# Feed-forward of one decoder layer: four more block pairs of up by two levels of block sums, and one-level pairs summed in PSUM

## The chip, the core and the metric

The kernel runs on one core of a Trainium2 chip. The time is that of the device for one execution, in microseconds (us). Before: a median of 1256.03 us over three runs (1255.54 to 1256.44). One further execution was profiled; every row of a profile or trace below is from it.

## The reference

One decoder layer on x of 1024 rows by 512 features, all in fp32: attention with 32 query heads and 8 key and value heads of 128 features, and then a gated feed-forward network with 1792 inner features. A normalisation follows each.

```python
x = layernorm(x + attention(x, wq, wk, wv, wo))
nx = x * rsqrt(mean(x * x) + 1e-5) * ln_w
g, u = nx @ gate_w.T, nx @ up_w.T          # 1024 x 1792 each
x = layernorm(x + (silu(g) * u) @ down_w.T)
```

## The kernel before

Attention comes first and takes the span up to about 1004 us. The change touches none of its instructions. What follows is the feed-forward part.

**Data.** `nT` holds the normalised rows turned, so that the 512 features lie on partitions (four chunks of 128) and the 1024 rows along the free axis. `hT[k]` holds inner features k x 128 to k x 128 + 127 for all rows: 14 blocks, first gate's output, then SiLU of it, then its product with up. `res` holds the rows before normalisation, in parts of the tiles `sums0` to `sums3`; the rest of these tiles serves as room for sums.

**One level.** The product of weights and `nT` is cut in two along each of three axes and computed with seven block products in place of eight (Strassen-Winograd). `blocks(m, ...)` loads the weights of inner block m and of block m + 7 (`far`), and GpSimd forms four sums of weight blocks. `lower` computes products 4 and 5 into the two banks of one tile of PSUM (`pair`, here `pb`), and `strassen` the other five. In the kernel before, each of these five has a bank of its own (`mbank`, four buffers): ScalarE copies product 1 to SBUF, and VectorE makes the four outputs of a pair of blocks with seven additions. A product is two matmuls of 128 x 128 x 512, each two instructions. The operands on the side of the rows are `s1` to `s4`, made on VectorE.

**Two levels.** `unit_blocks(m, ...)` loads the weights of four inner blocks (m, m + 1, m + 7, m + 8). GpSimd forms the sums of both levels. Each of the seven outer products, in the order k = 1, 2, 6, 7, 5, 3, 4, is a generator `stages` with seven matmuls of 128 x 128 x 256 in four steps. Step one fills a bank `c`, which ScalarE copies into `a` (both halves) and into `v`. Step two adds two products onto `a`, and ScalarE copies a half of `a` to `b`. Step three adds a third, and ScalarE copies that to the other half of `b`. Step four adds the last two, and VectorE sums `a`, `b` and `v` into `hT` or into four kept sums (`sa`, `sb`, `ua`, `ub`). Two of each three stages keep `a` and `b` in a `pair` tile, the third in two `mbank` tiles. The loop interleaves stages: step one of stage n, step two of n - 1, step four of n - 2, step three of n - 1. The operands on the side of the rows are in `x2`, which `inner_sums` fills on VectorE.

**Order.** Block 0 (with block 7) comes first, by one level, for gate and for up (`first_lower`, then `strassen` twice), while the last rows are still being normalised (`turn_norm`). Then gate's blocks follow in three units by two levels (m = 1, 3, 5). Then up's blocks follow in six pairs by one level (m = 1 to 6). In each pair ScalarE applies SiLU to gate's outputs after its copy of product 1, and GpSimd and VectorE multiply them by up. In pair 1 VectorE also scales `res` (eight operations, line 1518). From pair 2 on the weights of down are loaded, and GpSimd forms their sums (`weigh_rows`). Down comes last, by one level.

TensorE's instructions run in the order of the program (`keep_in_program_order`). A scheduler orders the other engines' queues as the kernel is built. Each engine works through its queue in order.

The rows of the profile name lines of the kernel before. Line 137 is the helper `matmul`. Lines 1111 (turned rows to `nT`), 1318 to 1328 (`strassen`), 1348 to 1350 (s2, s3, s4), 1369 to 1372 (`inner_sums`), 1414 to 1442 (`stages`), 1201 to 1245 (sums of weights), 1501 (SiLU) and 1503 (product with up) are those the text uses.

Of the kernel before, what the change touches and what calls it, by code (L numbers as in the profile page):

```python
# [28 lines left out]
F32 = mybir.dt.float32  # L29
# [67 lines left out]
def kernel(  # L97
# [47 lines left out]
    def mbank(name):  # L145
        return ps_m.tile([P, W], F32, tag="mbank", name=name)
# [4 lines left out]
    def rows(name):  # L151
        return wp.tile([P, W], F32, tag="w", bufs=3, name=name)

    def two_rows(name):
        return wp.tile([P, T], F32, tag="ww", bufs=4, name=name)
# [21 lines left out]
    mvs = const.tile([P, NT, 2], F32, tag="mvs", name="mvs")  # L177
    rs = const.tile([P, 2, NT], F32, tag="rs", name="rs")
# [7 lines left out]
    with ExitStack() as att:  # L186
# [494 lines left out]
        def pin(ins):  # L681

            if draining:
                tc.keep_in_program_order(ins)
# [419 lines left out]

        def turn_norm(k, n):
            i = ORDER[k]
            pt = mbank(f"nt_ps{i}").rearrange("p (c t) -> p c t", c=NC)
            for c in range(NC):
                turn(pt[:, c, :], n[:, c * P : (c + 1) * P])
            pin(  # L1110
                nc.vector.tensor_tensor(
                    nT[:, :, i * P : (i + 1) * P],
                    pt,
                    lnw.unsqueeze(2).to_broadcast([P, NC, P]),
                    ALU.mult,
                )
            )

# [52 lines left out]
    with ExitStack() as ffn:  # L1171
# [77 lines left out]
        def product(out, w, x):  # L1249
            for c in range(half):  # L1250
                matmul(
                    out,
                    lhsT=w[:, c, :],
                    rhs=x[:, c, :],
                    start=(c == 0),
                    stop=(c == half - 1),
                )
            return out
# [42 lines left out]
        kept_in = copied = None  # L1301

        def strassen(m, k, w, p5, p4, c11, c12, c21, c22):
            nonlocal copied
            b11, b21, b22, u1, u2, u3, u4 = w
            u = f"{k}_{m}"

            def bank(name):
                return mbank(f"{name}{u}")

            def kept(tag):
                if kept_in is None:
                    return rows(f"{tag}{u}")
                return kept_in.tile([P, W], F32, tag=tag, name=f"{tag}{u}")

            p1, p2 = product(bank("p1"), b11, a11), product(bank("p2"), b21, a12)
            v, v4 = kept("v"), kept("v4")
            copied = nc.scalar.copy(v, p1)
            nc.vector.tensor_tensor(c11, p2, v, ALU.add)
            p6 = product(bank("p6"), u2, s2)  # L1320
            nc.vector.tensor_tensor(v, p6, v, ALU.add)
            nc.vector.tensor_tensor(v4, p5, v, ALU.add)
            p7 = product(bank("p7"), u3, s3)
            nc.vector.tensor_tensor(v, p7, v, ALU.add)
            nc.vector.tensor_tensor(c22, p5, v, ALU.add)
            nc.vector.tensor_tensor(c21, v, p4, ALU.subtract)
            p3 = product(bank("p3"), b22, s4)
            nc.vector.tensor_tensor(c12, p3, v4, ALU.add)
# [25 lines left out]
        strassen(0, "g", wg, *pg, *hs)  # L1354
        for h in hs:
            nc.scalar.activation(h, h, AF.Silu)
        us = [fp.tile([P, T], F32, tag=f"h{k}", name=f"u{k}_0") for k in (6, 12)]
        us = [u[:, ts] for u in us for ts in (t0, t1)]
        strassen(0, "u", wu, *pu, *us)


# [3 lines left out]
        def inner_sums(r, to):  # L1365
            r11, r12 = r[:, :, 0, left], r[:, :, 0, right]
            r21, r22 = r[:, :, 1, left], r[:, :, 1, right]
            k1, k2, k3, k4 = (x2[:, to, k, :] for k in range(4))
            nc.vector.tensor_tensor(k1, r12, r11, ALU.subtract)
            nc.vector.tensor_tensor(k2, r22, k1, ALU.subtract)  # L1370
            nc.vector.tensor_tensor(k3, r22, r12, ALU.subtract)
            nc.vector.tensor_tensor(k4, r21, k2, ALU.subtract)

        by_half = nT.rearrange("p (n c) t -> p n c t", c=half)
        inner_sums(by_half[:, :, :, t0], slice(0, 2))
        inner_sums(ns[:, :4].rearrange("p n (c t) -> p n c t", c=half), slice(3, 7))
        inner_sums(by_half[:, 1:, :, t1], slice(2, 3))
# [8 lines left out]
        for h, u in zip(hs, us):  # L1386
            nc.gpsimd.tensor_tensor(h, h, u, ALU.mult)


        def stages(n, m, k, w, kept):  # L1390
# [28 lines left out]
            nc.scalar.copy(b[:, left], a[:, right])  # L1419
# [12 lines left out]
            def into(to_a, to_b, of_a, of_b):  # L1432
                add(to_a, a, of_a)
                add(halves(to_b), halves(of_b), twice(v))
                add(to_b, b, to_b)
# [4 lines left out]

            if k == 1:
                nc.scalar.copy(sa, a)
                add(halves(sb), halves(b), twice(v))
            elif k == 2:
                into(*h(0, t0), sa, sb)
            elif k == 6:
                into(sa, sb, sa, sb)
            elif k == 7:
                into(ua, ub, sa, sb)
            elif k == 5:  # L1450
                into(sa, sb, sa, sb)
                into(*h(1, t1), ua, ub)
            elif k == 3:
                into(*h(1, t0), sa, sb)
            else:
                into(*h(0, t1), ua, ub)
# [3 lines left out]
        inner = []  # L1460
        for m in (1, 3, 5):
            if m < 5:
                units.append(unit_blocks(m + 2, gate_t))
            for k in (m, m + 1, m + far, m + far + 1):
                hidden(k)
            for k in (1, 2, 6, 7, 5, 3, 4):
                inner.append(stages(len(inner), m, k, units[m // 2][k], kept))
                for back in (0, 1, 2, 1):
                    if back < len(inner):
                        next(inner[-1 - back])  # L1470
# [7 lines left out]
        kept_in = gp  # L1478
        wd, us = [], []
# [3 lines left out]
        def weigh_rows(c):  # L1483

            (b11, b12), (b21, b22) = ((w[:, :OH], w[:, OH:]) for w in (wd[c], wd[c + NI // 2]))
            u1, u2, u4 = (room.pop() for _ in range(3))
            nc.gpsimd.tensor_tensor(u1, b12, b11, ALU.subtract)
            nc.gpsimd.tensor_tensor(b12, b22, b12, ALU.subtract)
            nc.gpsimd.tensor_tensor(u2, b22, u1, ALU.subtract)
            nc.gpsimd.tensor_tensor(u4, b21, u2, ALU.subtract)  # L1490
            us.append((b11, b21, b22, u1, u2, b12, u4))

        for m in range(1, far):
            wu = blocks(m, "u", up_t)
            pu = lower(m, "u", wu)
            hs = [hT[k][:, ts] for k, ts in at(m)]
            ups = [gp.tile([P, W], F32, tag=f"g{n}", bufs=1, name=f"u{n}_{m}") for n in range(4)]
            strassen(m, "u", wu, *pu, *ups)
            with tc.issue_after(copied.ins):
                for h in hs:  # L1500
                    nc.scalar.activation(h, h, AF.Silu)
            for n, (h, u) in enumerate(zip(hs, ups)):
                (nc.gpsimd, nc.vector)[n % 2].tensor_tensor(h, h, u, ALU.mult)
            if m == 2:
                for t in [two_rows(f"wd{k}") for k in range(4)] + [piece(f"wd{k}") for k in (4, 5, 6)]:
                    wd += [t[:, :W], t[:, W:]]
                with tc.issue_after(loaded.ins):
                    for k in range(NI):
                        c = k // 2 + k % 2 * NI // 2
                        nc.sync.dma_start(wd[c], down_t[c * P : (c + 1) * P, :])  # L1510
            with tc.issue_after(summed.ins):
                for c in range((m - 2) * 2, (m - 1) * 2):
                    if 0 <= c < NI // 2:
                        weigh_rows(c)
            if m == 1:
                for k, i in enumerate(ORDER):
                    tc.keep_in_program_order(
                        nc.vector.tensor_scalar(
                            res[i],
                            res[i],  # L1520
                            mvs[:, k, 0:1],
                            rs[:, 0, k : k + 1],
                            ALU.subtract,
                            ALU.mult,
                        )
                    )
# [4 lines left out]
        for i in range(NT // 2):  # L1531
# [16 lines left out]
            def kept(tag):  # L1548
                bufs = 1 if tag == "v2" else None
                return gp.tile([P, W], F32, tag=tag, bufs=bufs, name=f"{tag}d{i}")[:, :OH]  # L1550
# [3 lines left out]
            p1s, v2, v4 = kept("v"), kept("v2"), kept("v4")  # L1554
# [118 lines left out]
```

## Time and profile before

| | |
|---|---|
| Median of three runs | 1256.03 us (1255.54 to 1256.44) |
| Profiled execution: time, span of its instructions | 1255.41 us, 1253.2 us |
| TensorE, VectorE, ScalarE, GpSimd busy in that span | 1235.6, 926.1, 491.8, 503.2 us |
| Mean granted clock of TensorE | 0.999 of full speed |
| Block 0, first matmul of `strassen` to the last | 1004.95 to 1022.38 us |
| Gate in units of two levels | 1022.38 to 1089.34 us |
| Up in pairs of one level | 1089.34 to 1161.44 us |
| Down, to the end of the span | 1161.44 to 1253.2 us |

In the rows PE is TensorE, DVE VectorE, ACT ScalarE, POOL GpSimd and PEld TensorE's weight load. A row of the timeline has the start, the duration, the engine, the line, the operation, output<-input and the count of instructions; in brackets stands the idle time of the engine before it and who ended it. A row of a matmul group covers its instructions from the first start to the last end, and the next group may start before that end, since matmuls are pipelined. A row of the waits has the engine that waited, what for, the time in total, how often, and the longest. A row of a window has the stretch, its length, the busy time and count of each engine, TensorE's granted clock, and the share and rate of the DMA engines.

### The profile page before, as it was taken

Reading aid. Unit: us, or ns where it says so; the run is one execution under the profiler, and the core shown is the slowest. Engines: PE = TensorE matmul, PEld = TensorE weight load, DVE = VectorE, ACT = ScalarE, POOL = GpSimd, SP = SyncE. Lnnn points to the kernel's source line nnn. Section 1 sums busy time; section 2 is a strip of 40 time slices with the busy share of each in tenths; the row PEclk is TensorE's granted clock in tenths of the full one; section 3 lists DMA queues with packets and bytes.
Section 4 is the critical chain, followed back from the end, with each engine's and each line's share of the span. In section 5 each row is a group of like instructions: output and inputs, shape, how many; then the busy total and the mean of one; then the engine's idle time right before and its main releaser. Section 6 shows DMA issues by size and latency. Waiting matters only on the chain. (4 is left out here: it accounts for less than half of the span.)

```text
span 1253.2 us, 14678 instructions
## 1 busy us (share of the span) xinstructions
PE 1235.6 (99%) x4252; PEld 754.9 (60%) x4252; DVE 926.1 (74%) x1876; ACT 491.8 (39%) x1000; POOL 503.2 (40%) x734
## 2 busy tenths in 40 slices
PE   9999999999999999999999999999999999999998
PEld 5645575565456755655567556554656758744887
DVE  5866887787788767877797678777765787577743
ACT  0443344444443444444444444454555135412000
POOL 4641434342424233425341424244320886386321
PEclk9999999999999999999999999999999999999999
DMA  8243325433444344334433433444444301510000
GB/s 277 51 118 80 84 65 145 103 88 79 130 97 100 79 119 100 93 82 123 99 86 85 131 83 84 120 117 110 112 103 113 92 17 36 167 51 1 17 18 34
DMA packets 86159, 115.56 MB, mean 92 GB/s; under 512 B 18368, under 2 KB 57024, under 8 KB 86080
## 3 DMA queue, kind: packets, MB, share of 16 engines
q1 hardware_dynamic: 85072, 112.66, 35.8%
q10 hardware_dynamic: 1008, 1.97, 0.4%
q8 instruction: 34, 0.56, 0.2%
q14 instruction: 45, 0.37, 0.1%
HBM read 37.23 MB, written 2.10 MB: 31 GB/s over the span
## 5 line engine op out<-in xcount | busy, mean ns | idle before, releaser
L609 ACT ACTIVATE p<-s,low 128x928 f32<-128x928 f32 (+31 forms) x256 | 179.1, 700 | 375.4 <-DVE low L589 363.2
L617 DVE STREAM_TRANSPOSE turned<-p 128x1024 f32<-128x1024 f32 (+7 forms) x244 | 187.3, 776 | 103.7 <-ACT p L614 70.8
L137 PE MATMUL o<-moved,v 128*128 128x512 f32 x550 | 254.6, 594 | 0.0
L614 ACT ACTIVATE p<-p,share 128x928 f32<-128x928 f32 (+31 forms) x256 | 188.0, 735 | 119.1 <-DVE share L613 119.0
L589 DVE CUSTOM_DVE_ANT_0 s<-s,mask 128x928 f32<-128x928 f32 (+31 forms) x256 | 179.1, 700 | 36.8 <-PE s L137 35.3
L137 PE MATMUL s<-k,queries 128*128 128x512 f32 (+15 forms) x576 | 204.0, 463 | 2.1 <-ACT p L609 2.1
L137 PEld LDWEIGHTS s<-k,queries 128*128 128x128 f32 x576 | 108.4, 190 | 110.5 <-issue 97.8
L137 PEld LDWEIGHTS o<-moved,v 128*128 128x128 f32 x550 | 102.4, 190 | 102.2 <-issue 95.1
L137 PE MATMUL q_p<-blocks,wq 128*128 128x512 f32 x260 | 124.5, 594 | 0.0
L604 POOL MEMSET p<- 128x96 f32 (+2 forms) x192 | 26.8, 150 | 229.4 <-DVE turned L617 208.6
L417 POOL TENSOR_TENSOR queries<-queries,q_b 128x512 f32<-128x512 f32 x52 | 71.4, 1372 | 114.9 <-DVE queries L416 106.0
L137 PE MATMUL y<-wo,oT 128*128 128x256 f32 x428 | 105.0, 382 | 0.7 <-ACT oT L847 0.7
L137 PEld LDWEIGHTS y<-wo,oT 128*128 128x128 f32 x428 | 79.4, 190 | 22.8 <-issue 7.9
L613 DVE RECIPROCAL share<-total 128x1 f32<-128x1 f32 x256 | 40.0, 156 | 61.3 <-ACT p L609 59.0
L411 DVE TENSOR_TENSOR q_b<-queries,sin 64x512 f32<-64x512 f32 x104 | 83.0, 798 | 3.1
L137 PEld LDWEIGHTS q_p<-blocks,wq 128*128 128x128 f32 x260 | 48.4, 190 | 45.9 <-issue 40.2
L137 PE MATMUL s<-kT,queries 128*128 128x512 f32 (+8 forms) x192 | 68.7, 466 | 1.9 <-ACT p L609 1.8
L772 DVE TENSOR_TENSOR sums<-y,sums 128x512 f32<-128x512 f32 x112 | 66.9, 606 | 3.5 <-PE y L137 2.3
L137 PEld LDWEIGHTS s<-kT,queries 128*128 128x128 f32 x192 | 35.7, 190 | 37.7 <-issue 28.9
L137 PE MATMUL y<-u,os 128*128 128x256 f32 x224 | 55.5, 384 | 0.7 <-POOL os L751 0.6
L137 PE MATMUL q_p<-blocks,uq 128*128 128x512 f32 x104 | 49.7, 592 | 0.0
L609 ACT ACTIVATION_READ_ACCUMULATOR p<-s,low 128x1 f32 x256 | 49.5, 193 | 0.0
(340 smaller groups left out, 1911.0 us busy)
## 6 DMA issues: line engine op xcount, KB each, us to landing
moved<-turned SPq DMA_DIRECT2D x112, 128.0 KB, 2.4
moved<-turned SPq DMA_DIRECT2D x128, 112.0 KB, 2.2
moved<-turned SPq DMA_DIRECT2D x112, 96.0 KB, 2.2
moved<-turned SPq DMA_DIRECT2D x112, 80.0 KB, 2.1
wo<-wo SPq DMA_DIRECT2D x16, 512.0 KB, 4.4
moved<-turned SPq DMA_DIRECT2D x128, 64.0 KB, 2.0
wq<-wq SPq DMA_DIRECT2D x14, 512.0 KB, 4.1
moved<-turned SPq DMA_DIRECT2D x128, 48.0 KB, 1.9
```

The source lines that it names most:

```text
L137: tc.keep_in_program_order(nc.tensor.matmul(*args, **kw))
L411: nc.vector.tensor_tensor(alike(b[0], dst)[to], dst[of], alike(sin[:, ts], dst)[of], ALU.mult)
L417: nc.gpsimd.tensor_tensor(dst, dst, alike(b[0], dst), ALU.add)
L589: extreme = nc.vector.tensor_tensor_reduce(out=s[:, :n], in0=s[:, :n], in1=mask[:, T - n :], scale=1.0, scalar=MASKED, op0=ALU.add, op1=AL ...
L604: cleared = nc.gpsimd.memset(p[:, n:full], 0.0)
L609: nc.scalar.activation(p[:, :n], s[:, :n], AF.Exp, bias=low, scale=-1.0, accum_out=total)
L613: nc.vector.reciprocal(share, total)
L614: last_of_all = nc.scalar.activation(p[:, :n], p[:, :n], AF.Copy, scale=share)
L617: nc.vector.transpose(x[:, :, :, b, :].rearrange("p b j q -> p j b q"), p[:, :full].rearrange("p (j b k) -> p j b k", b=B, k=Q),)
L772: pin(nc.vector.tensor_tensor(to, out, to, ALU.add))
```

## The change

1. Up's blocks 1 to 4 (with 8 to 11) are computed by two levels, in two more units of `stages` (m = 1 and 3). The products with gate's outputs follow in step four: on GpSimd for k = 2 and 3, on VectorE for k = 5 and 4. For k = 2 and 5 up's outputs stand in a pair of tiles `spare`. Pairs 5 and 6 remain by one level.
2. `strassen` adds products onto banks. Product 1 goes to a bank `a` and ScalarE copies it onto product 4's half of `pb` (`b`). Product 2 is added onto `a`, product 6 onto `b`. ScalarE copies `b` to `v`, product 3 is added onto product 5's half of `pb`, and product 7 onto `b`. ScalarE first copies products 5 and 4 to SBUF. VectorE has three additions (`put`), and for up the products with gate's outputs.
3. ScalarE scales `res` (`scale_residual`, with `nbs` = -mean x factor as bias), and applies SiLU to gate's outputs, one such task in each stage after the first copy of a half.
4. The inner sums of `nT` are issued after the last rows are turned, and block 0 of up after all inner sums in the text. The weights of down are loaded after those of pairs 5 and 6, and `weigh_rows` runs in these two pairs, with two of its seven rounds on VectorE.

```diff
-        def strassen(m, k, w, p5, p4, c11, c12, c21, c22):
+        def strassen(m, k, w, p5, p4, kept, hs, us=None):
...
-            p1, p2 = product(bank("p1"), b11, a11), product(bank("p2"), b21, a12)
-            v, v4 = kept("v"), kept("v4")
-            copied = nc.scalar.copy(v, p1)
-            nc.vector.tensor_tensor(c11, p2, v, ALU.add)
-            p6 = product(bank("p6"), u2, s2)
-            nc.vector.tensor_tensor(v, p6, v, ALU.add)
-            nc.vector.tensor_tensor(v4, p5, v, ALU.add)
-            p7 = product(bank("p7"), u3, s3)
-            nc.vector.tensor_tensor(v, p7, v, ALU.add)
-            nc.vector.tensor_tensor(c22, p5, v, ALU.add)
-            nc.vector.tensor_tensor(c21, v, p4, ALU.subtract)
-            p3 = product(bank("p3"), b22, s4)
-            nc.vector.tensor_tensor(c12, p3, v4, ALU.add)
+            def put(n, a, b, op=ALU.add):
+                to = us[n - 1] if us else hs[n]
+                nc.vector.tensor_tensor(to, a, b, op)
+                if us:
+                    nc.vector.tensor_tensor(hs[n], hs[n], to, ALU.mult)
+                else:
+                    nc.scalar.activation(to, to, AF.Silu)
+
+            nc.scalar.copy(v5, p5)
+            nc.scalar.copy(v4, p4)
+            a, b = mbank(f"pa{u}"), p4
+            product(a, b11, a11)
+            nc.scalar.copy(b, a)
+            product(a, b21, a12, True)
+            if us:
+                nc.vector.tensor_tensor(h11, a, h11, ALU.mult)
+            else:
+                nc.scalar.activation(h11, a, AF.Silu)
+            product(b, u2, s2, True)
+            copied = nc.scalar.copy(v, b)
+            product(p5, b22, s4, True)
+            put(1, p5, v)
+            product(b, u3, s3, True)
+            put(3, b, v5)
+            put(2, b, v4, ALU.subtract)
...
-            nc.scalar.copy(b[:, left], a[:, right])
+            done = nc.scalar.copy(b[:, left], a[:, right])
+            if tasks:
+                with tc.issue_after(done.ins):
+                    tasks.popleft()()
...
+            def end(to, of, rooms):
+                if not up:
+                    into(*to, *of)
+                    tasks.extend(lambda h=h: nc.scalar.activation(h, h, AF.Silu) for h in to)
+                    return
+                into(*rooms, *of)
+                for t, r in zip(to, rooms):
+                    (nc.gpsimd if k in up else nc.vector).tensor_tensor(t, t, r, ALU.mult)
...
+        tasks.extend(lambda k=k: scale_residual(k) for k in range(NT))
+        plan = [(m, gate_t, ()) for m in (1, 3, 5)] + [(1, up_t, (2, 3)), (3, up_t, (2, 3))]
...
-        for m in range(1, far):
-            wu = blocks(m, "u", up_t)
+        for m, wu in zip((5, 6), last):
             pu = lower(m, "u", wu)
```

## The prediction

> **What bounds the kernel now.** I read the page first, then TensorE's waits from 990 us on (the feed-forward part), then three windows of that part, then single rows.
>
> ```profile
> PE 1235.6 (99%) x4252; PEld 754.9 (60%) x4252; DVE 926.1 (74%) x1876; ACT 491.8 (39%) x1000; POOL 503.2 (40%) x734
> ```
>
> TensorE works 99% of the span, so a change pays only by removing matmul time or one of the few gaps:
>
> ```profile
> PE ab L137 <- ACT ab L1419: 2.1, 2, 1.8
> PE f L137 <- DVE hT L1503: 0.8, 1, 0.8
> PE p1g L137 <- DVE normed L1111: 0.8, 1, 0.8
> PE y L137 <- ACT oT L847: 0.7, 1, 0.7
> PE a L137 <- ACT b L1422: 0.5, 1, 0.5
> ```
>
> Only five gaps stand in 263 us. The reverse follows: a new wait of TensorE is paid in full. Three windows (columns PE, PEld, DVE, ACT, POOL) show the pairing block 0, a two-level unit of gate, and a one-level pair of up:
>
> ```profile
> 1004.00:1022.00 18.00, 17.21 (x41) 7.48 (x41) 17.96 (x20) 4.65 (x7) 12.94 (x11) 1.00 0.11 30
> 1043.00:1064.00 21.00, 21.00 (x99) 18.44 (x98) 14.78 (x23) 11.16 (x29) 14.01 (x16) 1.00 0.10 26
> 1117.00:1129.00 12.00, 12.00 (x29) 5.30 (x28) 5.62 (x9) 2.67 (x5) 11.84 (x15) 1.00 0.15 44
> ```
>
> VectorE is full in the first (17.96 of 18) and idle by half in the third.
>
> **Matmul time removed.** TensorE's starts:
>
> ```profile
> 1026.98 0.70 PE L137 MATMUL ab<-x,k 128*128 128x256 f32 x2 [1.78 <-ACT ab L1419]
> 1027.52 0.59 PE L137 MATMUL c<-ns,r 128*128 128x256 f32 x2
> 1027.95 0.59 PE L137 MATMUL c<-x,k 128*128 128x256 f32 x2
> 1092.78 1.88 PE L137 MATMUL p1u<-normed,wu 128*128 128x512 f32 x4
> 1094.49 1.88 PE L137 MATMUL p2u<-normed,wu 128*128 128x512 f32 x4
> ```
>
> A one-level product (four instructions) takes 1094.49 - 1092.78 = 1.716 us, a small one (two) 0.43. Two one-level pairs are 28 products, 24.0 us; a two-level unit is 49 small ones, 21.15. Two units of up (m 1 and 3) save 2 x 2.88 = **5.8 us**. The first row also shows what a wait adds: the next start comes 0.54 after it instead of 0.43, so 0.1 for starting again.
>
> **Waits added in each one-level pair.** Before, `strassen` gave p1, p2, p6, p7 and p3 banks of their own, and TensorE never waited. Now p2 is added onto p1's bank, p6 and p7 onto p4's, p3 onto p5's. In the built order of the changed kernel three matmuls of each pair carry a wait: p2 for ScalarE's copy b<-p1, p3 for ScalarE's copy v<-b, p7 for VectorE's sum that reads p5's half. The last two are bank neighbours in one pair tile, and the order guards the tile as a whole. Nothing lies between the two products, so nothing hides it.
>
> ```profile
> 1094.69 0.58 ACT L1318 COPY vu<-p1u 128x512 f32<-128x512 f32 x1 [6.43 <-PE p1u L137]
> 1098.13 0.69 DVE L1321 TENSOR_TENSOR vu<-p6u,vu 128x512 f32<-128x512 f32 x1 [0.95 <-PE p6u L137]
> ```
>
> p1 ends 1.88 after its start, 1094.66, and the copy starts 0.03 later. From p2's start of before to the copy's end is 1094.69 + 0.58 - 1094.49 = 0.78; with 0.07 back to TensorE (1088.40 against the copy's end 1088.26 gives 0.14, 1026.98 against 1026.93 gives 0.05) and 0.1 to start again it is 0.95. The VectorE sum gives 0.11 more, 1.06. So 0.95 + 0.95 + 1.06 = 2.96 a pair; **5.9 us** for m 5 and 6 (5.3 to 6.6 with the two latencies).
>
> **Block 0, gate.** Here the sum that p7 waits for is behind other work in VectorE's queue: in the built order it follows one `x2` sum, s2, s3, s4 and seven more `x2` sums. Rows of before for the same operations:
>
> ```profile
> 1006.13 1.74 DVE L1349 TENSOR_TENSOR ns<-normed 128x1024 f32<-128x1024 f32 x1
> 1009.47 1.21 DVE L1369 TENSOR_TENSOR x<-normed 128x512 f32<-128x512 f32 x1
> 1010.60 1.74 DVE L1369 TENSOR_TENSOR x<-ns 128x1024 f32<-128x1024 f32 x1
> 1015.26 1.21 DVE L1370 TENSOR_TENSOR x<-ns,x 128x1024 f32<-128x1024 f32 x1
> ```
>
> First a gain: before, four `x2` sums stood ahead of the turned block 0 (L1111 at 1004.21), which held p1 0.96 us. They move behind it, and the small `nbs` (under 0.2) fits in VectorE's wait for the transposes, so p1 starts at 1003.99. The block is written by 1003.15. Then VectorE needs 1.1 + 1.22 + 1.67 + 1.67 for the first four and 1.13 + 1.66 + 0.6 + 1.14 + 0.6 + 1.14 + 1.4 for the rest (starts, each 0.07 under its duration): the sum starts at 1016.5, and p7 at 1017.2. TensorE is there at 1003.99 + 4 x 1.716 + 2 x 0.95 = 1012.75. The wait is **4.4** (3.7 if each sum takes its shortest row, 5.3 if its longest). With p2 and p3 gate loses 4.5 + 1.9 = 6.4.
>
> **Block 0, up.** p2's copy stands on ScalarE behind three SiLU that wait for gate's last sums, and these stand on VectorE behind four 256-wide `x2` sums (3.4 us in before, 1.6 were each 0.4). p7g ends at 1019.1, the second of the sums at 1020.5 to 1021.7, then SiLU 0.55 and copy 0.58: p2 starts at 1022.1 to 1023.3, not 1020.65. I take 2.1, and 0.95 + 1.06: 4.1. Together block 0 ends 10.5 - 1.0 - 0.3 (its own restarts in before) = **+9.2 us** later (7.9 to 11.5).
>
> **Start of the two-level stages.** Before, VectorE freed `pbu` late and the stages lost 2.7 us (1.78 and 0.35, each with 0.16 of pipeline and 0.1 of restart). Now VectorE has three reads of it, not six, and is free 1.5 us after the first stage's start; 0.7 is left for the copies' own order. **-2.0** (-2.4 to -1.2).
>
> **Eight scalings and 24 SiLU on ScalarE.** One of 0.62 (L1501) in each stage, behind the copy of line 1419 and ahead of that of line 1422. There ScalarE stands idle:
>
> ```profile
> 1058.55 0.36 ACT L1422 COPY ab<-ab 128x256 f32<-128x256 f32 x1 [0.94 <-PE ab L137]
> ```
>
> 0.62 fits into 0.94: 0. In k = 1 a copy more stands there (0.58); if those five stages lose the overlap, 0.26 each, 1.3 us. A gain is excluded, since work is only added. The eight scalings that VectorE loses (7.0 us) lay in its idle half: 0.
>
> **First unit of up: GpSimd.** It must form the next unit's weights, and behind them in its queue stand two products h*u out of `spare`, which VectorE writes again at k = 5. Before, the same chain for gate's third unit ran
>
> ```profile
> 1047.84 1.26 POOL L1240 TENSOR_TENSOR r<-r,r 128x512 f32<-128x512 f32 x1 [6.81 <-PE ab L137]
> 1061.63 0.46 POOL L1235 TENSOR_TENSOR r<-r 128x128 f32<-128x128 f32 x1
> ```
>
> 5.3 us after the matmul that freed its buffer (1042.53), and 13.8 us to the last small sum. Now that matmul is 0.7 us before the unit starts (U): loads land at U + 4.6, four sums take 3.4, the chain 13.7, the two products 2.9 with a small sum between: U + 24.6. VectorE then has six operations to the freed bank (0.65 + 0.7 + 4 x 0.6) and ScalarE a copy, with 0.35 of latencies 4.7 in all: U + 29.3, where TensorE wants the bank at U + 25.0 (eight stages of seven small products, 3.02 each, and two more, 0.86). 29.3 - 25.0 is **+4.3**; it is 0 were GpSimd a fifth faster, and 5.5 with the chain's rows of 1.17 in place of 0.72 in three more places.
>
> **End of the second unit.** p4 of m = 5 takes the pair tile of the last stage but one; its release stands on VectorE behind ten sums of k = 5 and two row sums. From k = 5's last matmul to the end of the stages TensorE has 0.43 + 0.86 + 0.86 + 0.43 + 0.86 and one wait for a copy (0.65, as the 0.5 in the list above), 4.1 us; VectorE needs ten times 0.605 (start to start of such sums) and 0.26 of latencies, 6.3. Before, the last stage was on other banks and p4 followed at once (1089.34). 6.3 - 4.1 + 0.1 = **+2.3** (1.2 were the two products of k = 5 later, 3.4 at 0.7 a sum).
>
> **Down.** Its weights land late but GpSimd's sums of them (20 of 0.73 to 0.9, begun when the two-level stages end, 32 us ahead) are done some 9 us early (0); the 0.84 wait for hT (L1503) goes, since VectorE then has three operations after p7, 1.9 us, against 5.6 until TensorE asks: **-1.1** with pipeline and restart.
>
> **Sum:** -5.8 + 5.9 + 9.2 - 2.0 + 4.3 + 2.3 - 1.1 = **+12.8 us**. The profiled execution took 1255.41 (span 1253.2 and 2.2 around it), 0.6 under the median of 1256.03. So 1268.2 by this execution, 1268.8 against the median.
>
> [...] The two long waits (4.4 and 4.3) are longer than any in mid-kernel in before, where the clock stayed 1.00. The nearest row is the end of the span:
>
> ```profile
> 1235.00:1253.20 18.20, 12.31 (x58) 10.49 (x56) 6.52 (x18) 0.59 (x2) 2.42 (x3) 0.93 0.08 29
> ```
>
> TensorE is idle for the last 5.9 us and the mean granted clock is 0.93; what a matmul after such an idle time takes no row shows, so the sum charges the waits at their length. [...]
>
> **Rivals.** *The waits cost nothing* (other side): copies and sums are done when TensorE arrives. Then 5.8 + 1.0 + 2.0 + 1.1 = 9.9 us are saved: 1246. It decides from where twelve waits average under 0.8 us; rows of 0.58 and 0.69 plus latencies speak against it, and that p1 and p2 follow directly. 5%. *Only the plain waits*: VectorE's and GpSimd's queues keep up, 4 x 2.96 = 11.8 against 9.9: 1258, near no change. VectorE's 17.96 of 18 speaks against it. 8%. *GpSimd is in time*, the rest as forecast: 1264.5. 15%. *VectorE's and GpSimd's queues take their longest rows*: all high ends, up to 1276. 17%. The forecast itself: 55%.
>
> **Numbers.** What can be told from no change is 0.2%, 2.5 us. Faster comes from the first rival, no change from half of the second; all else is slower. The low ends of all terms, GpSimd in time, come to 5.1 us, 1261.1; the high ones, the 1.3 of ScalarE among them, to 20.2, 1276.2. That is the range; it leaves out the first two rivals.
>
> **What would show it.** Right: TensorE waits for ScalarE's b and v copies eight times at some 0.8, for VectorE's sum once at 4.2 and thrice at 0.9; one wait of some 4 in up's first unit, and one of 2 at p4 of m = 5; two-level units of 21.2. Wrong: p7g starting within 2 us of p3's end, no idle at p2 and p3, or ScalarE's added work delaying stages of gate.

## The result and the profile after

The changed kernel takes 1270.36 us (median of four runs, 1268.68 to 1270.85), against 1255.86 us for the kernel before (four runs beside them): a ratio of 1.0113, 95% interval 1.0095 to 1.0130. It is slower by 14.5 us. The profiled execution took 1270.63 us, with a span of 1268.6, 15.4 longer than before. Where these 15.4 lie, from the starts of matmuls in both timelines:

| Part | Before | After | Difference | Forecast |
|---|---|---|---|---|
| Start of block 0's `strassen` (p1 of gate) | 1004.95 | 1004.01 | -0.9 | -1.0 |
| Block 0, p1 of gate to the first two-level stage | 17.43 | 28.22 | +10.8 | +10.2 |
| Matmuls of up's blocks 1 to 4 | 48.05 | 42.30 | -5.8 | -5.8 |
| Waits of the two-level stages, up to p4 of pair 5 | 3.51 | 8.35 | +4.8 | +4.6 |
| Pairs 5 and 6 | 24.02 | 31.88 | +7.9 | +5.9 |
| Down | 91.76 | 90.39 | -1.4 | -1.1 |
| Sum | | | +15.4 | +12.8 |

(Stages are taken at 3.02 us and pairs of before at 12.01; the 42.30 is 14 stages. Forecast: block 0 is its 9.2 with the 1.0 of the earlier start taken out again. In the text p1 to p7 are the seven products, and p4 comes first in a pair of up.)

The page says first that TensorE's work has hardly grown while the span has (before: 1235.6, 99%):

```profile
PE 1238.4 (98%) x4336; PEld 772.2 (61%) x4336; DVE 928.3 (73%) x1885; ACT 524.5 (41%) x1074; POOL 505.9 (40%) x742
```

TensorE's waits from 990 us on (what waited, for what; total, count, longest):

```profile
PE pbg L137 <- DVE ns L1317: 3.7, 1, 3.7
PE pau L137 <- ACT pbu L1327: 2.6, 3, 1.2
PE pbu L137 <- DVE u L1317: 2.6, 3, 0.9
PE pbu L137 <- POOL us L1534: 2.0, 1, 2.0
PE ab L137 <- ACT ab L1421: 1.9, 1, 1.9
PE pbu L137 <- ACT v L1334: 1.4, 2, 0.7
```

The same list of before counted six waits, this one eighteen. Line 1327 is the copy b<-a, 1334 the copy v<-b, 1317 the sum in `put`. Up's three pairs each wait at p2, p3 and p7, as forecast. The list puts the 2.0 down to GpSimd's sums of down's weights (L1534), which end at the same moment. The eighth experiment moved them, and 1.83 of that wait stayed, now named after VectorE's sums of the stages. In the ninth pair 5 gets a tile that those sums give up a stage earlier, and the wait is gone: they are the cause.

The p2, p3 and p7 of gate's block 0 in the timeline, and the sum on VectorE that p7 waits for:

```profile
1006.61 1.98 PE L137 MATMUL pag<-normed,wg 128*128 128x512 f32 x4 [0.71 <-ACT pbg L1327]
1010.98 1.98 PE L137 MATMUL pbg<-ns,wg 128*128 128x512 f32 x4 [0.67 <-ACT vg L1334]
1016.67 3.59 PE L137 MATMUL pbg<-ns,tg 128*128 128x512 f32 x4 [3.70 <-DVE ns L1317]
```

```profile
1015.94 0.67 DVE L1317 TENSOR_TENSOR ns<-pbg,vg 128x512 f32<-128x512 f32 x1
```

VectorE reached that sum at 1015.94 without idling once from 1002.5 on; the forecast had 1016.5. What the forecast did not have stands in the duration of the third matmul row. This product lasts 3.59 us, the two above it 1.98 each: after the wait TensorE ran at half its clock (0.50 granted from 1016.52 to 1019.93). The granted clock is the third number from the end in these windows (start and end, length, busy time of PE, PEld, DVE, ACT, POOL, clock, DMA share and rate):

```profile
1013.11:1016.52 3.41, 0.00 (x0) 0.00 (x0) 3.41 (x5) 0.00 (x0) 0.00 (x0) 1.00 0.52 154
1016.52:1019.93 3.41, 3.26 (x4) 1.51 (x5) 1.52 (x5) 1.10 (x2) 0.00 (x0) 0.50 0.00 0
...
1118.92:1122.33 3.41, 1.52 (x8) 1.01 (x7) 3.41 (x5) 1.70 (x5) 2.93 (x4) 1.00 0.86 216
1122.33:1125.75 3.42, 3.42 (x10) 2.71 (x9) 3.29 (x7) 1.40 (x4) 2.52 (x2) 0.50 1.00 362
1142.81:1146.22 3.41, 1.10 (x4) 0.68 (x4) 3.41 (x7) 0.24 (x1) 1.84 (x3) 1.00 0.52 159
1146.22:1149.63 3.41, 3.31 (x4) 1.51 (x5) 3.41 (x4) 0.00 (x0) 3.41 (x4) 0.50 0.00 0
```

They come in twos: a stretch of 3.41 us in which TensorE works for less than half, then one of the same length at half clock. At a granted clock of 0.50 each of the three costs half of its length, 1.7 us: 5.1 in all (an estimate from the lengths).

### The profile page after: what moved, and what is told of

The parts are those of the page before. It is cut to its first block, busy times and chain, and to the rows that moved or that the text cites. A ratio compares the mean times of both kernels' runs of the same rounds, so it can differ in the third digit from the quotient of the medians.

```text
span 1268.6 us, 14945 instructions
## 1 busy us (share of the span) xinstructions
PE 1238.4 (98%) x4336; PEld 772.2 (61%) x4336; DVE 928.3 (73%) x1885; ACT 524.5 (41%) x1074; POOL 505.9 (40%) x742
## 6 DMA issues: line engine op xcount, KB each, us to landing
moved<-turned SPq DMA_DIRECT2D x128, 112.0 KB, 2.3
```

## The experiments

Each kernel ran beside the kernel before on the same chip. That one's median was 1254.7 beside experiments 1 to 4, 1255.72 beside 5 to 8, 1255.32 beside 9 and 10, and 1255.85 beside 11 and 12; the ratios are against these.

**1. Two-level units alone.** The old `strassen` (a bank for each product) is put back into the changed kernel, with block 0 in its old order:

```diff
-            a, b = mbank(f"pa{u}"), p4
-            product(a, b11, a11)
-            nc.scalar.copy(b, a)
-            product(a, b21, a12, True)
...
+            p1, p2 = product(bank("p1"), b11, a11), product(bank("p2"), b21, a12)
+            copied = nc.scalar.copy(v, p1)
+            nc.vector.tensor_tensor(c11, p2, v, ALU.add)
...
```

> Only the two-level units of up (parts 1, 3 and the late loads of down) on the old one-level pairs: every product of a pair in a bank of its own, block 0 and the inner sums in the old order. Theory A (the loss is in the pairs that share banks and in block 0): block 0 ends as before at 1022.4, pairs 5 and 6 take 12.0 us each, the two units bring -5.8, and the GpSimd wait in up's first unit (2.0 and a half-clock stretch of 1.7) and the wait ahead of pair 5 (2.2 and 1.7) stay: 1256 - 5.8 + 3.7 + 3.9 - 1.4 = 1256, 1252 if the clock does not fall. Rival B (the two-level units of up are themselves the loss, the sharing of banks is hidden): about 1270, as the whole change.

Measured 1259.94, ratio 1.0044 (1.0029 to 1.0059): 5.2 slower than before, where 0 was expected, and 9.3 faster than the whole change. Block 0 takes 17.27 us and pair 5 12.09 to the start of pair 6, with no waits: that half of the theory holds. The waits in up's first unit (2.50, with a half-clock stretch) and ahead of pair 5 (2.04) are there too. The miss is a new wait, in neither theory, at the start of down, with a half-clock stretch behind it:

```profile
1167.65 0.76 PE L137 MATMUL f<-wd,ns 128*128 128x256 f32 x2 [4.78 <-DVE u L1323]
```

VectorE owes pair 6's sums (L1323) there, and it had stood still before them:

```profile
1159.25 0.29 DVE L1560 TENSOR_TENSOR normed<-hT,hT 128x128 f32<-128x128 f32 x1 [4.97 <-POOL hT L1543]
```

It waited 4.97 us for two products h*u of pair 5 on GpSimd, which are queued behind the sums of down's weights. The changed kernel keeps these products on VectorE, so this wait is not in it.

**2. Pairs summed in PSUM alone.** The kernel before with only the new `strassen` (all six pairs of up and block 0) and SiLU as tasks in the stages; the edit is that of the change's first hunk.

> Only the one-level pairs summed in PSUM, in the six pairs of up and in block 0; up stays at one level, SiLU runs in the two-level stages as in the change, the residual's scaling stays on VectorE. Theory A: each pair takes 12.01 + 3.0 us, block 0 ends some 10 us later, the stages start 2 us better: 1256 + 6 x 3.0 + 10 - 2 = 1282. Rival B (the waits are hidden, the loss of the change is in the two-level units): 1256 to 1260. Rival C (only block 0 loses): about 1264.

Measured 1282.58, ratio 1.0221 (1.0206 to 1.0236): +27.9, as theory A had it, and rivals B and C fall. Its waits:

```profile
PE pbu L137 <- DVE u L1314: 6.0, 7, 0.9
PE pau L137 <- ACT pbu L1324: 5.3, 7, 1.0
...
PE pbu L137 <- ACT v L1331: 4.1, 6, 0.7
```

Six pairs of up and block 0's make seven. A pair in the middle takes 15.06 us (p4 to p4, 1144.55 to 1159.61): 3.05 over 12.01.

**3. Idle matmuls in the long waits.**

```diff
+            if k == "g":
+                idle = mbank(f"warm{u}")
+                for _ in range(2):
+                    product(idle, u3, s3)
             product(b, u3, s3, True)
...
+            for _ in range(4 if n == 29 else 0):
+                mm(c[:, left], l11, r11, True)
             mm(c[:, left], l11, r11, True)
...
+        idle = mbank("warm")
+        for n in range(4):
+            matmul(idle[:, left], lhsT=s1[:, 0, :P], rhs=s1[:, 0, left], start=True, stop=True)
```

> The changed kernel with idle matmuls, whose results nobody reads, in the three long waits of TensorE: two products (3.4 us) ahead of p7 of gate's block 0, four small ones (1.7 us) in stage 29, four (1.7 us) ahead of p4 of pair 5. Nothing else differs. Clock theory: the waits end when they ended before, the three stretches at half clock are gone, and with them 1.7 us each: 1265 to 1267. Rival: the half clock costs nothing, since VectorE or GpSimd sets the next wait anyway: 1270, with the next waits longer by what was saved.

Measured 1266.60, ratio 1.0095 (1.0080 to 1.0110). That is 11.9 over before, against 14.5 for the change: 2.6 less, though the kernel does more work. (The two profiled spans differ by 4.2, of which 0.6 lies ahead of block 0.) No stretch at half clock is left before TensorE's work has ended, and p7 of gate has its usual length:

```profile
1016.08 1.98 PE L137 MATMUL pbg<-ns,tg 128*128 128x512 f32 x4 [0.26 <-DVE ns L1317]
```

In block 0 the whole 1.6 is kept (26.61 us in place of 28.22). In the stages 1.0 of 1.7 is kept, in the pairs 1.0: a stage has a new wait of 0.90 for a copy, and p7 of pair 6 waits 1.53 for VectorE, not 0.92. So the clock theory holds for about 3.6 of 5.1 us; the other 1.5 come back as these two waits, for ScalarE's copy and VectorE's sum.

**4. GpSimd's two products to VectorE.**

```diff
-        plan = ... + [(1, up_t, (2, 3)), (3, up_t, (2, 3))]
+        plan = ... + [(1, up_t, (3,)), (3, up_t, (2, 3))]
```

> The changed kernel with up's two products of k = 2 in the first unit (m = 1) on VectorE in place of GpSimd. Theory A (VectorE's write of the spare room at k = 5 waits for these two products, which stand on GpSimd behind the sums of the next unit's weights): the wait of 1.9 us in stage 28 and the half clock behind it go, -3.7: about 1266.7. Rival: VectorE is behind by itself there and 1.3 us more on it make it worse: 1270 or more.

Measured 1268.46, ratio 1.0106 (1.0090 to 1.0123): 13.8 over before, 0.7 less than the change, so most of the expected 3.7 is missed. The wait of 1.9 and the half clock behind it are gone, and the way from the first stage to pair 5 is 112.0 us in place of 114.1. But 0.82 and 0.35 of new waits for copies stand nearby, and in this execution block 0 took 29.0, not 28.2, with half clock for 6.83 us. The mechanism is shown, its price is 2.1 in the place where it acts.

**5. All inner sums behind gate's block 0.**

```diff
-        with tc.issue_after(turned_norm.ins):
+        with tc.issue_after(gate_done.ins):
             inner_sums(by_half[:, :, :, t0], slice(0, 2))
-        inner_sums(ns[:, :4].rearrange("p n (c t) -> p n c t", c=half), slice(3, 7))
+            inner_sums(ns[:, :4].rearrange("p n (c t) -> p n c t", c=half), slice(3, 7))
...
```

Here `gate_done` is the last `put` of gate. The inner sums are twelve, not the eleven of the expectation.

> The changed kernel with all eleven inner sums behind gate's three sums of block 0 in VectorE's queue. Theory A (VectorE's whole work up to the first stage is the limit, the order only chooses which matmul waits): p7 of gate waits about 0.9 and runs at full clock, p7 of up waits 4 to 6 instead, and the first stage starts within 1.5 us of where it does in the changed kernel (28.2 us after p1 of gate). Rival (the place of the one sum in the queue is the whole cost): the first stage starts 22.5 to 24 us after p1 of gate, and the total falls by 4 to 5 us.

One run: 1277.52, before 1255.72. Both theories miss. p7 of gate waits only 0.85, as theory A said, but p7 of up then waits

```profile
1034.71 3.78 PE L137 MATMUL pbu<-ns,tu 128*128 128x512 f32 x4 [8.91 <-DVE u L1319]
```

and block 0 grows to 33.57 us. So the order does not merely choose who waits. Ahead of gate's three sums VectorE now stands idle for 5.57 and 2.08 us, and the inner sums, moved to a time when GpSimd forms weights, take longer. The same sum in the changed kernel, with GpSimd idle, and here, with GpSimd busy for 4.91 of the 4.99 us from its start on:

```profile
1011.93 1.21 DVE L1375 TENSOR_TENSOR x<-ns,x 128x1024 f32<-128x1024 f32 x1
```

```profile
1025.47 1.74 DVE L1378 TENSOR_TENSOR x<-ns,x 128x1024 f32<-128x1024 f32 x1
```

**6. Inner sums in VectorE's gaps.** Four stay ahead of gate's sums, four go between gate's and up's, the last four behind up's:

```diff
+        with tc.issue_after(gate_done.ins):
+            inner_sums(ns[:, :4].rearrange("p n (c t) -> p n c t", c=half), slice(3, 7))
...
+        with tc.issue_after(up_done.ins):
+            inner_sums(by_half[:, 1:, :, t1], slice(2, 3))
```

> The changed kernel with the inner sums put where VectorE is idle: four ahead of gate's sums of block 0, four between gate's and up's, the last four behind up's. Theory A: only the plain waits of the shared banks are left in block 0 (0.7, 0.7 and 0.9 in gate and in up), no half clock there, the first stage starts 23.1 us after p1 of gate instead of 28.2: 5 us less than the changed kernel, about 1265 beside 1256 for before, and nothing is given back in the first stages. Rival: VectorE is late afterwards, and 2 to 4 us come back as waits in the first six stages: 1268.

Measured 1265.35, ratio 1.0077 (1.0060 to 1.0094): 9.6 over before, 4.9 less than the change. Block 0 takes 23.84 us in place of 28.22 (23.1 was expected; p2 of up still waits 1.22), and from there to pair 5 it is 114.12 against 114.10: nothing is given back.

**7. Products 4 and 5 in different tiles.**

```diff
-            return [(pb[:, :W], pb[:, W:]) for pb in pbs]
+            return [(pbs[1 - n][:, :W], pbs[n][:, W:]) for n in range(2)]
...
-            p5 = product(pb[:, :W], w[3], s1)
+            p5 = product(mbank(f"p5{k}_{m}"), w[3], s1)
```

> The changed kernel with products 4 and 5 of a pair in different tiles of PSUM (block 0: crossed between gate's and up's pair tiles; pairs 5 and 6: product 5 in a bank of the other pool), so that a write of one no longer waits for a reader of the other. Theory A (the waits at p3 and p7 are only the shared guard of the pair tile): they vanish in pairs 5 and 6, which take 12.9 to 13.0 us each in place of 15.0; the wait of p2 stays at 0.7. In block 0 p7 of gate follows at once, and VectorE's backlog comes back at p2 of up (3 to 4 us). Total about 1260 to 1262 beside 1256. Rival (the copies and sums are needed by data): pairs stay at 15 us.

One run: 1262.25, before 1255.72, so some 8 less than the change. Pairs 5 and 6 take 13.07 and 12.98 us: the waits at p3 and p7 are gone, and with them 2.0 to 2.1 a pair; p2 still waits 0.70. They were waits for a neighbour in the tile, not for data. In block 0 the backlog comes back one step later, with its half clock, as theory A said:

```profile
1021.06 3.78 PE L137 MATMUL pau<-normed,wu 128*128 128x512 f32 x4 [4.64 <-ACT pbu L1327]
```

**8. Two-level units with the waits of experiment 1 taken out.** On that kernel:

```diff
-[(1, up_t, (2, 3)), (3, up_t, (2, 3))]
+[(1, up_t, (3,)), (3, up_t, (2, 3))]
...
-                (nc.gpsimd, nc.vector)[n % 2].tensor_tensor(h, h, u, ALU.mult)
+                last = nc.vector.tensor_tensor(h, h, u, ALU.mult)
...
+                if k == 5 and m == 3:
+                    put_off.append((to, rooms))
+                    return
```

(The products put off are issued after those of k = 4; `weigh_rows` is issued after `last`.)

> Two-level units of up on the old one-level pairs, as in the first experiment, with the waits that were found there taken out: products of k = 2 of the first unit on VectorE, products of k = 5 of the second behind the last reads of the stages, all products of pairs 5 and 6 on VectorE, and their sums of down's weights on VectorE behind them. Theory A: block 0 and the pairs wait nowhere, the wait ahead of down (4.8) and its half clock go, the wait in stage 28 is 0.5 to 1.2, that ahead of pair 5 under 1: 1249 to 1251 beside 1256, faster than before by 0.4 to 0.6%. Rival (VectorE has no room for the products that GpSimd gives up): 1254 to 1258.

Measured 1256.96 (ten runs), ratio 1.0010 (1.0001 to 1.0019). It reaches down at 1159.68, 1.8 earlier than before, and loses that there: 2.87 us of wait for VectorE's sums of down's weights, then 6.83 at half clock. (The profiled execution, 1258.44, is one of the slowest of the ten, which begin at 1254.91.) The wait ahead of pair 5 is still 1.83. The rival is right: waits moved.

**9. Three more moves.** On the eighth kernel, the last four inner sums go behind up's block 0, stage 32 takes a pair tile and 33 two banks, and the sums of down's weights leave the end of pair 6:

```diff
-            if n % 3 < 2:
+            if n % 3 < 2 and n != 33 or n == 32:
...
-                for c in range(4) if m == 5 else (4, 5, 6):
+                for c in (0, 1, 2, 3, 6) if m == 5 else (4, 5):
```

> The eighth experiment's kernel with three more moves: the last four inner sums behind up's sums of block 0; stage 32 in a pair tile and stage 33 in two banks, so that pair 5 takes over a tile that is free a stage earlier; the sums of down's weights that VectorE makes behind pair 6 now behind pair 5. Theory A: p1 of gate starts 1 us earlier, the wait at the start of the stages falls from 1.8 to under 0.8, that ahead of pair 5 (1.8) to under 0.4, that in down (2.9) and the half clock around it go: 1247 to 1250 beside 1256 for before, faster by 0.5 to 0.7%. Rival (each wait moves to the next late sum of VectorE): 1252 to 1256.

Measured 1254.02 (eleven runs), ratio 0.9990 (0.9980 to 0.9999): the one version that beats before, by about 1.3 us where 6 to 9 were expected; the rival's range held it. p1 of gate starts 1.3 earlier than in the eighth, the wait ahead of pair 5 is gone, no stretch at half clock is left before the end; the wait at the first stages stays 1.70, and pair 5's came back in part as 1.15 in stage 32. Down begins at 1158.83, 2.6 earlier than before, and takes 93.97 us in place of 91.76, with two waits for VectorE:

```profile
1166.21 0.70 PE L137 MATMUL f<-sums,hT 128*128 128x256 f32 x2 [1.61 <-DVE hT L1550]
1180.44 3.29 PE L137 MATMUL f<-wd,normed 128*128 128x256 f32 x14 [1.13 <-DVE v4d L1627]
```

**10. The change repaired.** Experiments 4, 6 and 7 together, the sums in PSUM kept.

> The changed kernel, its sums in PSUM kept, with three repairs together: products 4 and 5 in different tiles, inner sums placed as in the sixth experiment, products of k = 2 of the first unit on VectorE. Theory A (the shared guard, the place of the sums and the GpSimd queue are what the change lost beyond the one real wait at p2): only p2 waits in a pair (0.7 to 0.9, four times), the first stage starts 19.1 us after p1 of gate, pairs 5 and 6 take 13.0 us, up's first unit waits about 1.2: 1253 to 1256 beside 1256, no change or slightly faster. Rival (VectorE's backlog comes back at p2 of up as in the seventh experiment, with the half clock): 1258 to 1261.

Measured 1257.02 (ten runs), ratio 1.0014 (1.0005 to 1.0023): 1.7 over before, between the two theories' ranges. The wait of 2.04 ahead of pair 5 stays, with half clock behind it. Pairs 5 and 6 take 12.99 each without that half clock; block 0 takes 20.31, with p2 of up at 1.90, the end of VectorE's backlog. The three causes and their half clock are worth some 13 of the change's 14.5 us.

**11. Pair 6 alone summed in PSUM**, on the ninth kernel: `strassen` of the change with product 5 in a bank of the other pool.

> The ninth experiment's kernel with pair 6 alone summed in PSUM, products 4 and 5 in different tiles; pair 5 keeps a bank for each product. Theory A (the form that sums in PSUM costs one wait at p2, 0.9 with its restart, and gives VectorE less to do where it is late, ahead of down): pair 6 takes 13.0 us in place of 12.0, the waits in down (1.6 and 1.1) go to under 0.6 in all: 1252 to 1253, 1 to 2 us under the ninth. Rival (down's waits are not VectorE's backlog): 1255.

Measured 1255.04 (eleven runs), ratio 0.9998 (0.9989 to 1.0007): no gain over the ninth. Pair 6 takes 12.98, but down waits 2.01 for a product of pair 6, with a half-clock stretch behind it: the time is the rival's, but the waiting is still for VectorE.

**12. Two products of pair 6 on GpSimd**, on the ninth kernel:

```diff
-                last = nc.vector.tensor_tensor(h, h, u, ALU.mult)
+                e = nc.gpsimd if m == 6 and n % 2 == 0 else nc.vector
+                last = e.tensor_tensor(h, h, u, ALU.mult)
```

> The ninth experiment's kernel with two of the four products of pair 6 on GpSimd, which is idle there for 6.6 us, in place of VectorE. Theory A: VectorE is done 1.3 us earlier, the wait in down of 1.6 falls to 0.3 to 0.8 and the one of 1.1 to about 0.5: 1252.5 to 1253.5. Rival (a product of 1.3 to 1.7 us on GpSimd, and the differences of down behind it, end later than VectorE's): 1254 to 1256.

Measured 1256.58 (eleven runs), ratio 1.0008 (0.9999 to 1.0016): worse than the ninth, and a little above the rival's range. In the profiled execution, the slowest of the eleven (1258.43), down waits 0.48, 1.91 and 3.38. All three waits are for VectorE, not for GpSimd as the rival had it: VectorE is busy for 18.00 of the 18 us from 1157 to 1175, in the ninth for 15.47, though it has two products of pair 6 fewer. What a two-level up still loses on the way into down stays open; neither a shorter queue on VectorE in pair 6 nor GpSimd took it away.

## Why the prediction was right, step by step

**Matmul time removed.** 14 stages at 3.02 for four pairs at 12.01: -5.8, as forecast.

**Waits in each pair.** Forecast 2.96; measured 3.04 and 3.11 in pairs 5 and 6 (half clock taken out), and 3.05 in the second experiment. Which guard causes them was read from the built order and is shown by the seventh: 2.0 to 2.1 of the 3.0 are the shared tile, the remaining 1.0 is the copy b<-a, which must read the bank before p2 is added onto it.

**Block 0.** Gate lost 7.5 against 6.4, up 3.5 against 4.1. p7's wait was 3.7, not 4.4, since VectorE came 0.6 earlier; p2 of up waited 1.22. The forecast lacked the 1.7 us of half clock. The place of the sum in the queue was the right cause (sixth), but the fifth shows that not any other place helps.

**Start of the stages.** One wait of 0.50 in place of 1.78 and 0.35: about -1.9, forecast -2.0.

**ScalarE.** The scalings took 0.81, not the 0.62 that the forecast gave them, and still fit: no stage of gate waits after the first. The window of the unit between 1043 and 1064 us has TensorE full as before and ScalarE at 15.72 in place of 11.16:

```profile
1043.00:1064.00 21.00, 21.00 (x99) 18.37 (x98) 15.11 (x23) 15.72 (x36) 13.14 (x14) 1.00 0.17 51
```

**GpSimd in up's first unit** was the term with the largest error: 4.3 forecast, a wait of 1.9 measured. The fourth experiment shows that the two products on GpSimd cause it. The chain is the one described:

```profile
1115.42 1.26 POOL L1458 TENSOR_TENSOR normed<-normed,spare 128x512 f32<-128x512 f32 x1
```

```profile
1116.72 0.69 DVE L1440 TENSOR_TENSOR spare<-sums,sums 128x512 f32<-128x512 f32 x1 [3.30 <-POOL normed L1458]
```

The unit starts at 1093.73. GpSimd began its sums 3.3 us after that, not 4.6, and ended the products at 23.0, not 24.6; VectorE and the copy then took 4.5, not 4.7, and TensorE asked at 25.6, not 25.0.

**End of the second unit.** 2.0 ahead of pair 5, forecast 2.3. **Down.** -1.4, forecast -1.1.

**The clock** is the step that failed. The sum charged the long waits at their length, because no row of before showed a matmul after so long a wait in mid-kernel (its longest was 1.78 us). Three waits were each followed by 3.41 us at half clock, 5.1 us that the sum had at 0. The third was that ahead of pair 5, which the forecast did not count among the long ones. The total came out within 2 us of the measured median (2.6 in the profiled execution) all the same, because the rest came 2.5 us shorter than forecast: the error of the one hid about half of that of the other, and that is luck. Block 0, the two-level stages and the pairs each hold 1.7 us of half clock. Without it the table's 10.8, 4.8 and 7.9 would be 9.1, 3.1 and 6.2, against forecasts of 10.2, 4.6 and 5.9. In the 3.41 us ahead of each of the three stretches TensorE had been busy for 0.00, 1.52 and 1.10 us.

## What to carry to other kernels

Here products were added onto a bank that had just been copied, and with no other product between, the copy's latency stood on TensorE's path (0.70 us of wait at p2 of pairs 5 and 6 in the seventh experiment); two banks in one tile were guarded as one in the built order, so a product waited for the other bank's readers, which cost more (2 of 3 us a pair) than the one wait that the data asks for. VectorE was full around block 0 (3.41 of the 3.41 us ahead of p7's start) and had no free place in its queue: put into its gaps the sums cost 4.9 us less (sixth experiment), and moving them behind one consumer only starved the next (8.9 us in place of 3.7). Of the nineteen waits of TensorE between 1.8 and 3.4 us in these profiles twelve had half clock behind them, 1.7 us of loss for each stretch of the changed kernel (an estimate: half of its 3.41 us): put such a cost into the range, not at nothing. And read the built order of every engine, for what an edit moves in the queues was worth more here than what it saved in matmuls.

## What the hardware showed

Every figure here is from the profiles and runs of this case. The half-clock stretches of the changed kernel are 3.413 us long, and their starts lie whole multiples of that apart: 1016.52, 1122.33 and 1146.22 differ by 31 and 7 of them. The length of a wait alone did not decide. The wait of 2.03 us ahead of pair 5 was followed by half clock in the changed kernel (p4 lasted 3.60 us), but one of 2.04 us in the same place was not in the seventh experiment (1.96). There TensorE was busy a little more in the 3.41 us in which most of the wait lay, 1.54 us against 1.10:

```profile
1141.89:1145.30 3.41, 1.54 (x4) 0.85 (x5) 3.41 (x6) 0.00 (x0) 3.41 (x4) 1.00 0.16 60
```

In the twelfth, even a wait of 3.38 us had no half clock behind it. It fell across two stretches of 3.41 us, each busy for 1.67 us or more (they are placed, as an estimate, by counting back 25 and 24 such lengths from the half-clock stretch that starts at 1255.23, at the end of the span):

```profile
1169.90:1173.31 3.41, 1.67 (x8) 1.13 (x6) 3.41 (x11) 0.00 (x0) 2.67 (x6) 1.00 0.00 0
1173.31:1176.73 3.42, 1.78 (x8) 1.60 (x9) 2.92 (x14) 0.00 (x0) 0.62 (x1) 1.00 0.00 0
```

In all fourteen profiles, up to the end of TensorE's work, no wait under 1.8 us was followed by half clock, all five above 3.4 were (3.70 to 8.91 us), and of the nineteen between twelve were. The busy time of the 3.41 us does not give an exact border either. The 1.54 us above had full clock behind them; in the sixth experiment 1.55 had half:

```profile
1115.22:1118.63 3.41, 1.55 (x8) 1.28 (x8) 3.41 (x6) 2.06 (x6) 2.58 (x4) 1.00 0.94 253
1118.63:1122.05 3.42, 3.42 (x10) 2.71 (x9) 3.29 (x6) 1.04 (x3) 2.87 (x3) 0.50 0.95 343
```

In the changed kernel 1.52 had half clock behind them, too. In the kernel before, the wait of 1.78 left 1.89 of its 3.41 us busy, with full clock behind. The number of stretches also fits the scatter of the changed kernel, though only one of its executions was profiled: its fastest run (1268.68) has a mean clock of 0.997, the three others (1270.09 to 1270.85) 0.995, and one stretch lowers the mean by 0.0013 (half of 3.413 in 1268.6 us).

A half-clock stretch of 3.41 us in which TensorE was busy for 2.77 us (eighth experiment, from 1167.69) was followed by another one, a stretch busy for 2.80 us (tenth, from 1136.84) by full clock.

Some sums of VectorE and GpSimd took longer where both engines worked at the same time: 1.74 us above for a sum of VectorE, with GpSimd busy for 4.91 of 4.99 us, against 1.21 for the same sum with GpSimd idle, and 1.70 for GpSimd's sums of 128x256 with VectorE busy, against 0.72 with VectorE idle. No experiment changed this alone, so that one slows the other is not shown. The changed kernel's own trace has the two lengths for GpSimd:

```profile
1004.16 1.70 POOL L1235 TENSOR_TENSOR k<-r 128x256 f32<-128x256 f32 x1
1024.26 0.72 POOL L1235 TENSOR_TENSOR k<-r 128x256 f32<-128x256 f32 x1
```

VectorE is busy throughout the first (1.70 of 1.70 us) and idle during the second (0.00 of 0.72). So a sum that was moved in time had another price here, 1.74 us in place of 1.21.
